# The second half of a block's turned sums: from one VectorE instruction to a ScalarE copy and two GpSimd additions

## The chip, the core and the metric

The kernel runs on one core of a Trainium2 chip. The metric is the device time of one execution in microseconds, of which the median over several runs is taken. A core has five engines that run their own instruction streams side by side: TensorE (PE in the profile; its weight loads have a row of their own, PEld), VectorE (DVE), ScalarE (ACT), GpSimd (POOL) and SyncE (SP), which here only issues DMAs. An engine waits for another by a semaphore.

## What is computed

A decoder layer with three parts, each followed by a row-wise layer normalisation, on x of 16 x 256 rows of 256 numbers, all in float32:

```python
def attn(residual, w_fc, w_proj, ln_g, ln_b):
    x = layernorm(residual, ln_g, ln_b)
    q = x.reshape(Bx, Tx, 4, 64).transpose(0, 2, 1, 3)
    k = w_fc.reshape(-1, 64)
    v = w_proj.T.reshape(-1, 64)
    p = square(relu(einsum('bhtd,sd->bhts', q, k)))
    out = einsum('bhts,sd->bhtd', p, v)
    return residual + out.transpose(0, 2, 1, 3).reshape(Bx, Tx, Cx)
...
x = _layernorm(x + attn(x, ...))
x = _layernorm(x + xattn(x, ctx, fraction, ...))
x = _layernorm(x + ffn(x, ...))
```

The change lies in the first part. Its result before the normalisation is x + (x + out), that is, 2x plus the attention's sums. The second part is an attention of 16 heads over a context, with a bias made from the clipped differences of a fraction; the third a feed-forward layer with eight experts that add a low-rank term. They stay as they are.

## The kernel before, in words

The 4096 rows are cut into NB = 8 blocks of 512. A tile of rows has 128 partitions and four groups of 256 numbers (j = 0 to 3). The order of instructions is written out by hand (`manual_schedule`, from line 949): each engine executes its instructions in the order in which the program issues them.

**Stage one** (lines 973 to 1047, about the first 250 us) is the first part, block after block. In a block TensorE alternates between score steps and values steps. A step m of the eight issues two calls of `scores` (line 334), then the two calls of `values` (line 351) that belong to the scores of the step before, then what the list `steps[m]` holds. A call of `scores` makes four matmuls (eight instructions in the profile, L339) into a ps_a tile, which has two banks of PSUM; ScalarE takes its relu into SBUF (L347), VectorE squares it (L348), and a step later the values matmuls (L358) read it. There are two ps_a buffers, so the relu of one call must have read a buffer before the call after next may write it. Calls of `scores` in a block: 16.

The values are summed in PSUM. `keep` (line 366) takes the sums out after the fourth and the eighth step: a ScalarE copy (L367), another (L372) into `half`, and a GpSimd addition of the two (L373). The sums have channels on the partitions and rows along the free axis; they must be turned.

**The seam between two blocks** is the list `turning` (lines 1004 to 1008, run at 1044): the next block's normalised x is turned in two parts, `turn_in(0)` with a ScalarE eviction (L324) and `turn_in(1)` with a VectorE eviction (L329), and between the two stands `turn_rows` (line 399) for the block before the one that just ended. `turn_rows` takes a ps_a tile, makes two generators of `turn_out` (line 375), one for each half jj of the rows and each with one bank of the tile, and steps them: four transposes for each half (L384), then for each half the eviction at L390, one VectorE instruction that computes 2x + sums from PSUM into y. So the order on TensorE at a seam is: four transposes, eight, four, and the next block's first score step. The seams behind blocks 1 to 6 have a `turn_rows`, for blocks 0 to 5. The seam behind block 0 has none. Blocks 6 and 7 are turned later, in stage two, by `turn_out` without a tile (lines 1088 and 1111).

What reads y: its row statistics in steps 1 and 2 of the next block (`measure_out`, line 406, bn_stats at L185), and `norm_out` (line 410) from step 7 on, a ScalarE scaling into hid (L245) and a GpSimd addition (L413).

The x tiles have three buffers. `nxt.load` in step 0 (line 1001, DMA at L256 on SP's queue) brings the block after into the buffer of the block that was just turned, so it waits until that block's evictions have read x. Behind it on SP's queue stand a row of fractions (L442) and the store of a clipped difference (L553), which VectorE makes at L534 in step 0 and in step 5 of blocks 2 to 6. The loaded x is measured by VectorE in steps 3 and 4.

**Stage two** (from line 1068) runs the attention over the context and the feed-forward part in one hand-made order. The change has no instruction there.

Of the kernel before, what the change touches and what calls it, by code (L numbers as in the profile page):

```python
# [11 lines left out]
ALU = mybir.AluOpType  # L12
# [10 lines left out]
def tile_decoder_layer(ctx: ExitStack, tc: tile.TileContext, a: dict, out: bass.AP):  # L23


    nc = tc.nc
# [23 lines left out]
    def tile_b():  # L50

        if turns:
            turns[0] += 1
            if turns[0] % 3 == 0:
                return psV.tile([P, 512], FP, tag="W", name="ps_b")
        return psB.tile([P, 512], FP, tag="B", name="ps_b")
# [175 lines left out]
    if True:  # L232
# [16 lines left out]
        class Block:  # L249
# [125 lines left out]
            def turn_out(self, jj, ps=None):  # L375
                if self.tb >= NB - 2:
                    self.y = hid[:, 4 * self.tb : 4 * self.tb + 4, :]
                elif jj == 0:
                    self.y = p1.tile([P, 4, C], FP, tag="y", name="y")
                if ps is None:  # L380
                    ps = tile_b()
                for j in range(2):
                    for c in range(CC):
                        nc.tensor.transpose(  # L384
                            ps[:, j * C + c * P : j * C + (c + 1) * P],
                            self.oT[:, c, (2 * jj + j) * P : (2 * jj + j + 1) * P],
                            ident,
                        )
                yield
                nc.vector.scalar_tensor_tensor(  # L390
                    self.y[:, 2 * jj : 2 * jj + 2, :].rearrange("p j c -> p (j c)"),
                    self.x[:, 2 * jj : 2 * jj + 2, :].rearrange("p j c -> p (j c)"),
                    2.0,
                    ps,
                    ALU.mult,
                    ALU.add,
                )
# [551 lines left out]
    with tc.manual_schedule():  # L949
# [23 lines left out]
        for tb in range(NB):  # L973
# [58 lines left out]
            for m in range(8):  # L1032
                c, n2 = divmod(m, 4)
# [34 lines left out]
        for n in range(N + 2):  # L1068
# [135 lines left out]
            if n in measured:  # L1204
                j = measured.index(n)
                row_stats(hid[:, 4 * (NB - 1 - j // 4) + j % 4, :], rest_mv[:, j, :])
            if n in LATE:
                j = LATE.index(n)
# [120 lines left out]
```

## Time and profile before

| | us |
|---|---|
| median of 3 runs | 899.75 (899.52 to 900.03) |
| the profiled execution | 900.11 |
| its span in the trace | 898.3 |
| L348 DVE, squares, 128x1024, x128 | 153.9 busy, 1243 ns mean |
| L390 DVE, evictions into y, 128x512, x12 | 7.7 busy, 684 ns mean |
| L367 and L372 ACT, copies from PSUM, 128x512 | 587 and 592 ns mean |
| L373 POOL, additions, 128x512, x15 | 19.1 busy, 1273 ns mean |
| L413 POOL, additions, 128x256, the 24 of stage one | 723 to 1766 ns, median 1655 |
| POOL busy from 80 to 240 us, by 40 us | 10.2, 11.0, 12.3, 14.6 |

A row of a group gives its line, engine and operation, the tiles that it writes and reads (out<-in), the shape, the count, then busy microseconds and the mean of one in nanoseconds, then the engine's idle time before it and what ended it. A row of the timeline gives the start and the length in microseconds from the span's start; instructions that follow each other closely are merged and counted (x2), and what stands in brackets is the idle time before and its releaser. Score and values steps stand there as x16. The granted TensorE clock is 0.998 of the full one over the execution.

### The profile page before, as it was taken

To read this page: it belongs to the slowest core of one execution; us is meant where nothing else is said; L and a number is where in the kernel's file an instruction comes from. 1 tells how busy PE (TensorE), PEld (TensorE's weight loads), DVE (VectorE), ACT (ScalarE), POOL (GpSimd) and SP (SyncE) were. 2 spreads that over 40 slices of the span, in tenths; PEclk is the share of its full clock that TensorE was granted. 3 is DMA by queue.
4 is the path that set the end of the run, shared out by engine and by line. 5 is a ranking of instruction groups with operands and counts; after the bars stand their busy time and mean duration, and the time that the engine had idled before them with its cause. 6 is when DMAs were issued, how large, how long until landed. Compare 5 with 4: busy or idle time off the path is not lost.

```text
span 898.3 us, 19061 instructions
## 1 busy us (share of the span) xinstructions
PE 887.4 (99%) x6940; PEld 560.8 (62%) x6940; DVE 713.1 (79%) x1986; ACT 567.3 (63%) x951; POOL 398.5 (44%) x385
## 2 busy tenths in 40 slices
PE   8999999999999999999999999999999999999997
PEld 4334444444466777577668757766875786586555
DVE  6879899988779999778777877877798787778344
ACT  5766777777787888376656836666684665556111
POOL 1100223422489998435534644563464456344010
PEclk9999999999999999999999999999999999999999
DMA  5501110110001222011111102011110201111001
GB/s 140 154 1 42 53 42 26 30 49 1 14 1 55 70 69 57 14 42 23 34 49 39 47 14 67 20 37 45 43 48 14 66 20 37 43 28 43 23 2 46
DMA packets 44190, 37.01 MB, mean 41 GB/s; under 512 B 14912, under 2 KB 40000, under 8 KB 44096
## 3 DMA queue, kind: packets, MB, share of 16 engines
q1 hardware_dynamic: 43520, 35.52, 14.5%
q8 instruction: 55, 0.90, 0.4%
q14 instruction: 39, 0.32, 0.1%
q10 hardware_dynamic: 576, 0.26, 0.1%
HBM read 21.07 MB, written 6.03 MB: 30 GB/s over the span
## 4 chain that ended last, share of the span: by engine, by line
PE 97%; DVE 1%; ACT 1%; issue 0%; POOL 0%; DVEq 0%; ACTq 0%; POOLq 0%
PE ps_b L689 13%; PE ps_a L339 13%; PE ps_v L358 12%; PE ps_l L884 12%; PE ps_l L649 8%; PE ps_b L914 7%; PE ps_v L705 7%; PE ps_v L914 5%; PE ps_b L601 3%; PE ps_b L497 3%; PE ps_b L471 3%; PE ps_b L519 3%; PE ps_l L896 2%; PE ps_b L811 1%; PE ps_b L458 1%; PE ps_b L796 1%
## 5 line engine op out<-in xcount | busy, mean ns | idle before, releaser
L628 POOL TENSOR_SCALAR neg<-dneg,aneg,delta 128x512 f32<-128x512 f32 x217 | 182.9, 854 | 181.8 <-PE ps_b L689 127.4
L664 DVE CUSTOM_DVE_ANT_0 neg<-ps_l,neg 128x256 f32<-128x256 f32 x512 | 181.5, 420 | 26.5 <-PE ps_l L649 22.6
L640 ACT ACTIVATE ps_l<-dpos,apos_d 128x512 f32<-128x512 f32 x256 | 172.9, 687 | 40.3 <-DVE mx L664 35.6
L696 ACT ACTIVATE pT<-ps_b 128x512 f32<-128x512 f32 x256 | 142.4, 591 | 59.3 <-PE ps_b L689 57.2
L348 DVE TENSOR_TENSOR pr<-pr 128x1024 f32<-128x1024 f32 x128 | 153.9, 1243 | 30.2 <-ACT pr L347 29.8
L347 ACT ACTIVATE pr<-ps_a 128x1024 f32<-128x1024 f32 x128 | 124.9, 1025 | 52.9 <-PE ps_a L339 52.5
L689 PE MATMUL ps_b<-ident,neg 128*128 128x128 f32 x1024 | 138.5, 277 | 2.0 <-ACT pT L696 1.8
L689 PEld LDWEIGHTS ps_b<-ident,neg 128*128 128x128 f32 x1024 | 113.6, 141 | 35.9 <-issue 12.4
L679 POOL TENSOR_TENSOR neg<-neg,mx 128x1024 f32<-128x1024 f32 x65 | 124.2, 1911 | 18.2 <-DVE mx L664 17.0
L339 PE MATMUL ps_a<-xnT,kT 64*64 64x512 f32 x1024 | 124.6, 593 | 1.0 <-ACT xnT L324 0.4
L358 PE MATMUL ps_v<-pr,vv 64*64 64x512 f32 x1024 | 122.7, 589 | 0.0
L884 PE MATMUL ps_l<-xt,wi 128*128 128x512 f32 x248 | 111.5, 595 | 0.0
L679 DVE TENSOR_TENSOR neg<-neg,mx 128x1024 f32<-128x1024 f32 x63 | 99.2, 1575 | 0.6
L413 POOL TENSOR_TENSOR hid<-hid,bo 128x256 f32<-128x256 f32 x32 | 43.7, 1367 | 105.3 <-ACT hid L245 86.5
L358 PEld LDWEIGHTS ps_v<-pr,vv 64*64 64x64 f32 x1024 | 45.2, 133 | 64.4 <-issue 54.5
L339 PEld LDWEIGHTS ps_a<-xnT,kT 64*64 64x64 f32 x1024 | 42.0, 133 | 65.2 <-issue 52.7
L649 PE MATMUL ps_l<-kM,qT 32*128 32x256 f32 x1024 | 75.9, 401 | 0.0
L884 PEld LDWEIGHTS ps_l<-xt,wi 128*128 128x128 f32 x248 | 45.3, 190 | 49.0 <-issue 44.4
L373 POOL TENSOR_TENSOR xt<-xt,half 128x512 f32<-128x512 f32 x15 | 19.1, 1273 | 120.3 <-ACT half L372 120.3
L914 PE MATMUL ps_b<-wof,hT 128*128 128x256 f32 x304 | 68.4, 380 | 0.0
L705 PE MATMUL ps_v<-pT,vaug 128*32 128x256 f32 x1024 | 66.4, 384 | 0.0
L907 DVE TENSOR_SCALAR hT<-ps_l,wib 128x512 f32<-128x512 f32 x43 | 29.8, 746 | 43.9 <-PE ps_l L896 43.9
(131 smaller groups left out, 1087.3 us busy)
## 6 DMA issues: line engine op xcount, KB each, us to landing
cT<-in_ctxT SPq DMA_DIRECT2D x16, 256.0 KB
kM<-keys SPq DMA_DIRECT2D x128, 32.0 KB
v<-raw SPq DMA_DIRECT2D x128, 32.0 KB
invs<-rows SPq DMA_DIRECT2D x128, 32.0 KB
x<-in_x SPq DMA_DIRECT2D x7, 512.0 KB
out<-x SPq DMA_DIRECT2D x7, 512.0 KB
frow<-in_frac SPq DMA_DIRECT2D x16, 128.0 KB
wi<-in_wiT SPq DMA_DIRECT2D x1, 1024.0 KB
```

Source lines behind the costliest of these rows:

```text
L339: nc.tensor.matmul(sc[64 * k : 64 * k + 64, h, :], lhsT=kT[64 * h : 64 * h + 64, q, hf * P + 64 * k : hf * P + 64 * k + 64], rhs=self.xnT[ ...
L348: nc.vector.tensor_tensor(pr, pr, pr, ALU.mult)
L358: nc.tensor.matmul(self.acc[k][64 * h : 64 * h + 64, :], lhsT=vv[64 * k : 64 * k + 64, hf, 64 * q : 64 * q + 64], rhs=pr[64 * k : 64 * k + ...
L628: nc.gpsimd.tensor_scalar(self.neg[:, g], self.batch.dneg, aneg[:, h : h + 1], delta, ALU.mult, ALU.mult,)
L640: nc.scalar.activation(banks[g], self.batch.dpos.rearrange("p j k -> p (j k)"), AF.Copy, scale=apos_d[:, h : h + 1],)
L649: nc.tensor.matmul(banks[g][:, j * S : (j + 1) * S], lhsT=self.batch.qT[rows, self.o, j * P : (j + 1) * P], rhs=self.batch.kM[rows, self.i ...
L664: nc.vector.tensor_tensor_reduce(out=self.t[:, g, j, :], in0=banks[g][:, j * S : (j + 1) * S], in1=self.neg[:, g, j, :], scale=1.0, scalar ...
L679: eng.tensor_tensor(rows, rows, top.to_broadcast([P, 4, S]), ALU.subtract)
L689: nc.tensor.transpose(ps[:, k * S + j * P : k * S + (j + 1) * P], self.t[:, g, j, k * P : (k + 1) * P], ident,)
L696: nc.scalar.activation(self.pT[:, g, :], self.ps[g], AF.Exp)
L884: nc.tensor.matmul(self.banks[g], lhsT=wi[:, c, f * P : (f + 1) * P], rhs=self.xT[:, c, :], start=(c == 0), stop=False,)
L914: nc.tensor.matmul(ps[:, 0:C], lhsT=self.hT[f][:, j * P : (j + 1) * P], rhs=wof[:, f, :], start=(f == 0), stop=(f == FC - 1),)
```

## The change

`turn_out` remembers whether it took its own PSUM tile. If it was handed one and turns the second half (jj = 1), ScalarE copies the turned sums from PSUM into the two row groups of y, and GpSimd adds x to them twice, in place. The first half, and every call without a tile, keep the VectorE instruction.

```diff
+                own = None
                 if ps is None:
-                    ps = tile_b()
+                    ps = own = tile_b()
                 for j in range(2):
                     for c in range(CC):
                         nc.tensor.transpose(
...
                 yield
+                if ps is not own and jj == 1:
+
+                    rows = self.y[:, 2:4, :].rearrange("p j c -> p (j c)")
+                    nc.scalar.copy(rows, ps)
+                    for _ in range(2):
+                        nc.gpsimd.tensor_tensor(
+                            rows, rows, self.x[:, 2:4, :].rearrange("p j c -> p (j c)"), ALU.add
+                        )
+                    return
                 nc.vector.scalar_tensor_tensor(
                     self.y[:, 2 * jj : 2 * jj + 2, :].rearrange("p j c -> p (j c)"),
                     self.x[:, 2 * jj : 2 * jj + 2, :].rearrange("p j c -> p (j c)"),
```

## The prediction

> **What bounds the kernel now.** I read the page first, then the chain of waits inside stage one, then the timeline around the seams between two blocks of stage one, where the changed lines run.
>
> ```profile
> span 898.3 us, 19061 instructions
> PE 887.4 (99%) x6940; PEld 560.8 (62%) x6940; DVE 713.1 (79%) x1986; ACT 567.3 (63%) x951; POOL 398.5 (44%) x385
> ...
> PE 97%; DVE 1%; ACT 1%; issue 0%; POOL 0%; DVEq 0%; ACTq 0%; POOLq 0%
> ```
>
> TensorE is busy 99% of the span and is 97% of the chain that ended last. So work taken from DVE is worth nothing by itself: only time that TensorE loses counts. A busy PE row can hide such a loss, because the ends of matmuls are modelled. So I compare starts. In the steady part of a block two score steps (x16 in the timeline: eight matmul instructions each) start 1.71 us before the values that follow them (74.08 to 75.79). At a seam it is longer. The seam into the third block, with the turned sums in it:
>
> ```profile
> 70.05 1.29 DVE L390 SCALAR_TENSOR_TENSOR y<-x,ps_a 128x512 f32<-128x512 f32 x2 [0.25 <-PE ps_a L384]
> 70.37 0.21 PEld L339 LDWEIGHTS ps_a<-xnT,kT 64*64 64x64 f32 x8 [0.17 <-issue]
> 70.38 2.19 PE L339 MATMUL ps_a<-xnT,kT 64*64 64x512 f32 x16
> ...
> 71.45 0.24 PEld L339 LDWEIGHTS ps_a<-xnT,kT 64*64 64x64 f32 x8 [0.87 <-issue]
> 71.53 2.12 ACT L347 ACTIVATE pr<-ps_a 128x1024 f32<-128x1024 f32 x2 [1.58 <-PE ps_a L339]
> ...
> 72.36 1.93 PE L358 MATMUL ps_v<-pr,vv 64*64 64x512 f32 x16
> ```
>
> and the seam into the second block, the only one without turned sums:
>
> ```profile
> 37.85 1.95 PE L339 MATMUL ps_a<-xnT,kT 64*64 64x512 f32 x16 [0.43 <-ACT xnT L324]
> ...
> 39.62 1.90 PE L358 MATMUL ps_v<-pr,vv 64*64 64x512 f32 x16
> ```
>
> The reader is to see 72.36 - 70.38 = 1.98 us in the first and 39.62 - 37.85 = 1.77 us in the second: 0.21 us lost. The place is the weight load at 71.45. The seam's tile of turned sums is one of the two ps_a buffers. The block's first score step takes the other, its second this one, and so waits until both L390 evictions have read it. They end at 70.05 + 1.29 = 71.34; the load follows 0.11 us later. The view says "issue" there, but the eviction's end is the only event that fits. The last such seam gives the same (219.21 to 221.19, 1.98). Six seams lose 6 x 0.21 = 1.26 us.
>
> **The change, part by part.** The new branch needs a tile handed in and jj = 1. Only turn_rows hands one in, for blocks 0 to 5: six times. Blocks 6 and 7 call turn_out without one and stay as they are. Each time one DVE L390 goes (684 ns), and one ScalarE copy and two GpSimd additions of 128x512 come.
>
> *Removed, on the path.* With one eviction left DVE ends at 70.05 + 0.68 = 70.73.
>
> *Added, ScalarE.* The nearest row is the copy of 128x512 from PSUM at L372, 592 ns. In program order it stands behind the eviction of turn_in(0) (69.17 + 0.78 = 69.95) and ahead of the relus. It can start when DVE now starts, about 70.06, and ends at 70.65. Behind it waits the relu at 71.53, which sat idle 1.58 us for TensorE: 0.59 of that is filled, 0.9 left. Both readers are done by 70.73, where the second score step would come at about 71.24: cover 0.5 us. The stall of 0.21 goes. Next late is TensorE itself. If ScalarE were 0.6 us later than this, the stall would be back.
>
> *Added, GpSimd.* Two additions like this one:
>
> ```profile
> 74.82 0.59 ACT L372 COPY half<-ps_v 128x512 f32<-128x512 f32 x1
> ...
> 75.49 1.26 POOL L373 TENSOR_TENSOR xt<-xt,half 128x512 f32<-128x512 f32 x1 [16.52 <-ACT half L372]
> ```
>
> It starts 0.08 us after ScalarE's copy, so mine run 70.73 to 72.0 and, with the same 0.08 between them as an estimate, 72.08 to 73.35. The queue ahead is free (an L413 addition ends at 219.2 ahead of the last seam), and the next in it is L373 at 75.49. The rule that speaks against this step is the Trainium skill's, "GPSIMD Engine Reference", section 3.1: an addition there costs about 2.6 cycles per element against VectorE's one, so elementwise work belongs on VectorE. From its 2.6 and 1.2 GHz, 512 elements give an estimate of 1.11 us plus dispatch, near the row's 1.26. As a cost on the path it would be 2 x 1.26 + 0.59 - 0.68 = 2.43 us a seam, 14.6 us in all. By the trace nothing on the path waits for these rows: their readers are the row statistics of measure_out(1) at 82.22, 8.9 us after 73.35. I take zero.
>
> *Moved, the load of x.* The next block's x (512 KB, at 71.40, just after the second eviction) goes into the buffer that the additions read. SP now issues it at about 73.4, 2.0 us later, and with it what stands behind: frow (71.82, read one block later) and nothing urgent, as the store of dneg comes at 75.58. The DMA columns by microsecond show x landed at about 75.1, so it will be about 77.1. Its first reader is at 85.55: 8 us of cover. Zero.
>
> *Shared with DVE.* This is the doubtful part. The squares at L348 run beside the second addition. The rows are
>
> ```profile
> 73.73 1.22 DVE L348 TENSOR_TENSOR pr<-pr 128x1024 f32<-128x1024 f32 x1
> 74.86 0.69 DVE L534 CUSTOM_DVE_ANT_1 dneg<-frow,nfcol 128x512 f32<-128x512 f32 x1
> 76.37 1.47 DVE L348 TENSOR_TENSOR pr<-pr 128x1024 f32<-128x1024 f32 x1 [0.82 <-ACT pr L347]
> ```
>
> and, from the answer on line 413, the spread of an addition of half the size that often meets squares:
>
> ```profile
> L413 POOL TENSOR_TENSOR hid<-hid,bo x24: 723/1655/1766, 98.6 to 251.1; 128x256 f32<-128x256 f32 x24
> ```
>
> The square at 76.37 overlapped L373 by 0.38 us and took about 0.27 longer; L413 goes from 723 to 1655 ns. The Trainium skill, "SBUF — State Buffer", section "Who interferes with whom", says that a VectorE instruction with two SBUF inputs and a GpSimd one that reads SBUF exclude each other: the later one waits until the earlier ends. DVE's remaining L390 and L329 read one operand from PSUM and should not be touched; at 99.81 an L390 beside an L413 shows no lengthening.
>
> After the change the first square is ready at 72.59 and the second addition ends at 73.35. By the rule it waits 0.76; by the row's proportion (0.27 for 0.38) it loses 0.54. It ends at 74.4 to 74.6 and the next at 75.5 to 75.7. Their values matmuls start at 75.58 and 76.44 (0.21 earlier than now): room 1.0 and 0.75. Nothing by either.
>
> In the next step L373 (ready at 75.28, held by the second square until about 75.6) runs to 76.9, the clip at L534 stands ahead of the third square. If the clip is not held, the squares end at 78.0 and 79.15 against values at 79.01 and 79.87. If it is (its two inputs are in SBUF; no row shows one meeting an addition), they end at 78.65 and 79.85: the last has no room, and I put 0.1 us on TensorE. Five seams have a clip, so the cost lies between zero and 0.5 us. I take 0.1, nearer zero, because L373 at 75.49 touched the clip's end and stayed at its own 1.26.
>
> **Sum.** -1.26 + 0.1 = -1.16 us, rounded to -1.2. The profiled execution took 900.11 us (span 898.3 and 1.8 around it): it would become 898.9. The median of the runs shown is 899.75, which gives **898.55 us**. TensorE sets stage two as well, so the shift should reach the end whole.
>
> **Rivals.**
> *The port decides* (slower). The two additions and L373 hold DVE one after another. The place is the fourth square after a seam; from its end to its values matmul there is now 80.08 - 78.98 = 1.10 us, less the 0.11 from an end to a load: 1.0. Up to 0.76 comes from the second addition and 0.3 to 1.0 from L373 and a clip pushed into it: 1.1 to 1.8 in all, and from 1.0 on TensorE stands. In the middle 1.45 - 1.0 = 0.45, and as the stop comes 0.21 earlier, 0.66 us a seam: 5 x 0.66 - 1.26 = +2.0, **901.8 us**. For it: L413 more than doubles beside squares, and DVE has little room in the next steps (two squares 2.36 and two row statistics 1.15 in a step of 3.43). Against: it needs every hold at its end.
> *The stall stays*: the second score step gets another wait, on ScalarE's copy or on two semaphores, as late as the old one. For it: the row was called "issue". Against: the 0.5 us of cover. **899.75 us**.
> *DVE's relief counts in full*: 6 x 0.684 = 4.1 us, **895.6 us**. For it: DVE is at 8 to 9 tenths in stage one. Against: DVE is 1% of the chain.
> That the change does not do what it says is no rival beyond the count: six blocks of eight.
>
> **How the numbers follow.** A measurement of this kernel can tell about 0.2% from no change, 1.8 us: 897.95 and 901.55 are the bounds. My forecast 0.70, all but 0.02 of it within them; the stall stays 0.12, within; DVE's relief 0.05, faster; the port 0.13, slower. So faster 0.07, same 0.80, slower 0.13. The range runs from 897.9 (the forecast and half a microsecond) to 900.3 (the stall stays, with half a microsecond of holds), and leaves out about 0.2.
>
> **What would show it.** Right: at six seams score steps to values in 1.77, not 1.98; the second load no longer behind L390; the copy at 0.59 ended before 71; POOL additions near 1.27, twice six; x issued 2 us later with the statistics unmoved; first squares longer by 0.5 to 0.8. Wrong: values matmuls starting late in the first or second step after a seam (the port), or a second load still 1.08 us behind the first.

## The result, and the profile after

The changed kernel takes **904.0 us** (903.5 to 904.39, five runs) against 899.75 before: a ratio of 1.0048, interval 1.0037 to 1.006. It is slower by 4.25 us, outside the range that was given. The page of the changed kernel, span and busy rows, the chain by engine, the squares, and the addition of `keep`:

```profile
span 902.2 us, 19076 instructions
PE 889.1 (99%) x6940; PEld 548.4 (61%) x6940; DVE 725.4 (80%) x1980; ACT 571.8 (63%) x957; POOL 421.6 (47%) x397
...
PE 89%; DVE 7%; issue 2%; ACT 2%; POOL 0%; DVEq 0%; ACTq 0%; POOLq 0%
...
L348 DVE TENSOR_TENSOR pr<-pr 128x1024 f32<-128x1024 f32 x128 | 164.4, 1326 | 23.7 <-ACT pr L347 23.6
...
L373 POOL TENSOR_TENSOR xt<-xt,half 128x512 f32<-128x512 f32 x15 | 25.7, 1717 | 83.6 <-ACT half L372 83.6
```

VectorE lost six instructions of 684 ns and is nevertheless busy 12.3 us longer: a busy row counts the time in which an instruction is held. The squares went from 1243 to 1326 ns, 10.5 us in all, the addition at L373 from 1273 to 1717. TensorE still reads 99%, but the chain gave 8 points from it to others, 6 of them to VectorE. Of these rows only the chain's says that TensorE now waits for others; the size of the loss is in none of them.

Where it lies is read from the starts of the blocks, the first score step of each on TensorE. Blocks 3 and 4 before:

```profile
100.14 0.66 PE L339 MATMUL ps_a<-xnT,kT 64*64 64x512 f32 x4
...
129.91 0.66 PE L339 MATMUL ps_a<-xnT,kT 64*64 64x512 f32 x4
```

and after:

```profile
99.67 0.66 PE L339 MATMUL ps_a<-xnT,kT 64*64 64x512 f32 x4
...
130.44 0.66 PE L339 MATMUL ps_a<-xnT,kT 64*64 64x512 f32 x4
```

From block 3 to block 7 before: 100.14, 129.91, 159.68, 189.44, 219.21, so 29.77 us each. After: 99.67, 130.44, 161.22, 191.98, 222.75, so 30.77. Block 2 takes 29.74 after, 29.77 before. From the last block's start to the start of the last score call it is 28.24 against 27.66, and what follows takes 651.2 against 651.4. So four blocks lost 1.0 us each and block 7 lost 0.6; block 2 and stage two lost nothing.

The seam into block 2 in the changed kernel, from the timeline (lines of the file moved by one to ten: L400 is the old L390, L544 the clip, L423 the old L413; L394 and L396 are the new copy and the new additions):

```profile
69.60 0.69 DVE L400 SCALAR_TENSOR_TENSOR y<-x,ps_a 128x512 f32<-128x512 f32 x1 [0.25 <-PE ps_a L385]
...
69.93 2.12 PE L339 MATMUL ps_a<-xnT,kT 64*64 64x512 f32 x16
...
70.21 0.80 DVE L329 TENSOR_SCALAR xnT<-ps_b,ln_g,ln_b 128x512 f32<-128x512 f32 x1
...
70.32 0.59 ACT L394 COPY y<-ps_a 128x512 f32<-128x512 f32 x1 [0.81 <-DVE y L400]
...
70.98 3.51 POOL L396 TENSOR_TENSOR y<-y,x 128x512 f32<-128x512 f32 x2 [12.46 <-ACT y L394]
...
71.87 1.90 PE L358 MATMUL ps_v<-pr,vv 64*64 64x512 f32 x16
...
72.14 3.43 DVE L348 TENSOR_TENSOR pr<-pr 128x1024 f32<-128x1024 f32 x2 [1.13 <-ACT pr L347]
...
74.99 1.73 POOL L373 TENSOR_TENSOR xt<-xt,half 128x512 f32<-128x512 f32 x1 [0.49 <-ACT half L372]
...
75.50 1.76 DVE L544 CUSTOM_DVE_ANT_1 dneg<-frow,nfcol 128x512 f32<-128x512 f32 x1
```

Three things are to be seen. First, the copy waits for VectorE's eviction (it ends at 70.29) instead of running beside it. So ps_a is free only at 70.91, 0.98 us behind the block's first score step, where it was 0.96 before (71.34 - 70.38). The seam takes 71.87 - 69.93 = 1.94 us, 0.04 less than before and not 0.21; even this little comes only because the next score call follows the copy's end after 0.05 us, where it followed VectorE's after 0.15. Second, the two additions take 3.51 us, not 2.6: taken one by one the second lasts 2.15, and the two squares 1.23 and 2.29. An instruction is called held here when its row grows to about the end of another engine's instruction that it overlaps. The first square holds the second addition until about 73.3, and that holds the second square until 74.5. Third, the same happens with the next pair: L373 waits for the second square (1.73 for 1.27) and holds the clip (1.76 for 0.69). VectorE is then 2.2 us behind where these instructions alone would put it.

Almost nothing stops in block 2, because the squares had room. The fourth square there, and the values matmuls that read it:

```profile
78.32 1.21 DVE L348 TENSOR_TENSOR pr<-pr 128x1024 f32<-128x1024 f32 x1
```

```profile
79.59 1.08 PE L358 MATMUL ps_v<-pr,vv 64*64 64x512 f32 x8
```

It ends 0.06 us ahead of them, where the kernel before had 1.1. The seam has used up the room, and no more. One step into a later block, block 4, the rows of three engines:

```profile
137.82 1.68 POOL L423 TENSOR_TENSOR hid<-hid,bo 128x256 f32<-128x256 f32 x1 [0.59 <-ACT hid L245]
```

```profile
138.84 1.75 DVE L348 TENSOR_TENSOR pr<-pr 128x1024 f32<-128x1024 f32 x1
```

```profile
140.64 1.09 PE L358 MATMUL ps_v<-pr,vv 64*64 64x512 f32 x8 [0.36 <-DVE pr L348]
```

L423 is the addition of the row bo in `norm_out`, here called a bo addition. It holds the fourth square for 0.53 us, and TensorE waits for that square: here is the stop, 0.54 us against block 2. It is about half of what the block loses. The rest follows in the same way, 0.05 us in the next step and 0.4 in the one behind it:

```profile
145.16 1.70 POOL L423 TENSOR_TENSOR hid<-hid,bo 128x256 f32<-128x256 f32 x1 [3.29 <-ACT hid L245]
```

```profile
148.00 1.09 PE L358 MATMUL ps_v<-pr,vv 64*64 64x512 f32 x8 [0.20 <-DVE pr L348]
```

Blocks 3 to 7 have such additions in steps 1 to 3, block 2 has none. Before the change they cost nothing: block 2 took 29.77 us there as well as the others.

### The profile page after: what moved, and what is told of

Same layout as the page of the kernel before. It is cut to its first block, busy times and chain, and to the rows that moved or that the text cites. A ratio compares the mean times of both kernels' runs of the same rounds, so it can differ in the third digit from the quotient of the medians.

```text
span 902.2 us, 19076 instructions
## 1 busy us (share of the span) xinstructions
PE 889.1 (99%) x6940; PEld 548.4 (61%) x6940; DVE 725.4 (80%) x1980; ACT 571.8 (63%) x957; POOL 421.6 (47%) x397
## 4 chain that ended last, share of the span: by engine, by line
PE 89%; DVE 7%; issue 2%; ACT 2%; POOL 0%; DVEq 0%; ACTq 0%; POOLq 0%
PE ps_b L699 13%; PE ps_l L894 12%; PE ps_v L358 8%; PE ps_a L339 8%; PE ps_l L659 8%; PE ps_b L924 7%; PE ps_v L715 7%; PE ps_v L924 5%; DVE pr L348 4%; PE ps_b L611 3%; PE ps_b L507 3%; PE ps_b L481 3%; PE ps_b L529 3%; PE ps_l L906 2%; PE ps_b L821 1%
## 5 line engine op out<-in xcount | busy, mean ns | idle before, releaser
L348 DVE TENSOR_TENSOR pr<-pr 128x1024 f32<-128x1024 f32 x128 | 164.4, 1326 | 23.7 <-ACT pr L347 23.6
L423 POOL TENSOR_TENSOR hid<-hid,bo 128x256 f32<-128x256 f32 x32 | 37.7, 1180 | 107.0 <-ACT hid L245 88.2
L358 PEld LDWEIGHTS ps_v<-pr,vv 64*64 64x64 f32 x1024 | 38.0, 132 | 76.5 <-DVE pr L348 36.4
L339 PEld LDWEIGHTS ps_a<-xnT,kT 64*64 64x64 f32 x1024 | 37.3, 133 | 69.5 <-issue 50.9
L373 POOL TENSOR_TENSOR xt<-xt,half 128x512 f32<-128x512 f32 x15 | 25.7, 1717 | 83.6 <-ACT half L372 83.6
```

The lines of the kernel that those rows point to most:

```text
L339: nc.tensor.matmul(sc[64 * k : 64 * k + 64, h, :], lhsT=kT[64 * h : 64 * h + 64, q, hf * P + 64 * k : hf * P + 64 * k + 64], rhs=self.xnT[ ...
L348: nc.vector.tensor_tensor(pr, pr, pr, ALU.mult)
L358: nc.tensor.matmul(self.acc[k][64 * h : 64 * h + 64, :], lhsT=vv[64 * k : 64 * k + 64, hf, 64 * q : 64 * q + 64], rhs=pr[64 * k : 64 * k + ...
```

## The experiments

Theory P: the loss comes from GpSimd's additions and VectorE's two-input instructions excluding each other. Its sharper form R: the seam's additions only use up the squares' room; what stops TensorE are the bo additions that then meet late squares. Rivals: S, the copy on ScalarE and its late release; W, GpSimd's work in proportion; B, the backlog of VectorE by itself. In the cuts of code `rows`, `x_rows` and `y_rows` stand for the two row groups of the half in question.

**VectorE adds instead of GpSimd**

```diff
-                    for _ in range(2):
-                        nc.gpsimd.tensor_tensor(rows, rows, x_rows, ALU.add)
+                    nc.vector.scalar_tensor_tensor(rows, x_rows, 2.0, rows, ALU.mult, ALU.add)
```

> The change with its two GpSimd additions replaced by one VectorE instruction (2x + the copied rows, both in SBUF); the ScalarE copy stays. Theory P (the loss comes from GpSimd's additions and VectorE's squares shutting each other out of SBUF): no L373 and no clip longer than before, squares back at 1243 ns mean, no stop of TensorE at values; the seam from scores to values stays at the changed kernel's 1.94 us against 1.98, so 899.75 - 6 x 0.04 = 899.5 us. Theory S (the copy on ScalarE and its later release of ps_a cost the time): still about 904.

Measured: 900.9 us, ratio 1.0014 (1.0007 to 1.0021). The copy stayed and most of the loss is gone, so S does not hold, but it is 1.4 us over what P expected. Blocks 3 to 6 take 30.18. Its rows in step 1 of block 3, GpSimd and VectorE, each from its engine's timeline:

```profile
106.44 0.72 POOL L423 TENSOR_TENSOR hid<-hid,bo 128x256 f32<-128x256 f32 x1 [0.95 <-ACT hid L245]
```

```profile
106.49 1.75 DVE L348 TENSOR_TENSOR pr<-pr 128x1024 f32<-128x1024 f32 x1
```

and the same two in the kernel before:

```profile
107.58 1.76 POOL L413 TENSOR_TENSOR hid<-hid,bo 128x256 f32<-128x256 f32 x1 [1.05 <-ACT hid L245]
```

```profile
107.54 1.21 DVE L348 TENSOR_TENSOR pr<-pr 128x1024 f32<-128x1024 f32 x1
```

Before, the square comes 0.04 us ahead and GpSimd waits (1.76), which costs nothing, as nobody waits for that row. Here the addition comes 0.05 ahead and the square is held to 1.75. The clip had delayed L373 by 0.1, that the third square, that the fourth: 0.1 us decides which side pays. This square still had room (1.02 us, now 0.48). The next two bo additions hold a square in the same way, and only there TensorE stops, by 0.05 and 0.43 us. The second stop:

```profile
116.02 1.09 PE L358 MATMUL ps_v<-pr,vv 64*64 64x512 f32 x8 [0.20 <-DVE pr L348]
```

**The same without the bo additions of steps 1 to 3**

```diff
-                eng.tensor_tensor(rows, rows, bo, ALU.add)
+                if eng:
+                    eng.tensor_tensor(rows, rows, bo, ALU.add)
```

> The run with the VectorE addition in place of GpSimd's (900.9 us) without the bo additions to row groups 1 to 3 in steps 1 to 3 (those rows lack bo). That run lost 0.41 us in each of blocks 3 to 6, where its fourth square was held 0.53 us by a bo addition that in the kernel before comes 0.04 us too late to hold it. Theory R: without these additions its blocks take 29.70 us, about 899.1 us. If the VectorE addition itself costs the time: 900.9 stays.

Measured: 899.2 us, ratio 0.9996 (0.9987 to 1.0004); the blocks take 29.70. The 1.7 us between the two runs belong to the bo additions' holds.

**One addition** (the second half's rows lack one x)

```diff
-                    for _ in range(2):
+                    for _ in range(1):
```

> The change with one GpSimd addition of x instead of two, so that the second half's rows are x + sums and not 2x + sums. Theory P by place: the one addition runs from 70.98 to 72.25, the first square comes at 72.14, so nothing is held but 0.1 us; time as in the run with the VectorE addition, 899.5 us. Theory W (GpSimd's work costs in proportion): half of the 4.25 us stays, about 901.9 us.

Measured: 899.0 us, ratio 0.9993 (0.9984 to 1.0001). W falls: half of the work costs none of the loss. The timelines of GpSimd and VectorE show the single addition ending about as the first square begins, and both squares at their own length:

```profile
100.69 1.28 POOL L396 TENSOR_TENSOR y<-y,x 128x512 f32<-128x512 f32 x1 [1.04 <-ACT y L394]
```

```profile
101.85 2.36 DVE L348 TENSOR_TENSOR pr<-pr 128x1024 f32<-128x1024 f32 x2 [1.13 <-ACT pr L347]
```

**Two further additions in the kernel before**

```diff
+                if own is None and jj == 1:
+                    spare = p1.tile([P, 2 * C], FP, tag="spare", bufs=1, name="spare")
+                    nc.gpsimd.tensor_tensor(spare, y_rows, x_rows, ALU.add)
+                    nc.gpsimd.tensor_tensor(spare, spare, x_rows, ALU.add)
```

> The kernel before, both evictions on VectorE, with two further GpSimd additions of 128x512 into a spare tile after each of the six seams; nothing reads the result. Theory P: the second addition waits for the first square and then holds the second one, L373 is held by that and holds the clip, as in the changed kernel: 904 to 905 us, squares at a mean near 1326 ns. Theory S (the ScalarE copy and the y that comes late cost the time): nothing waits for the spare tile, about 900 us.

Measured: 905.6 us, ratio 1.0066 (1.005 to 1.0083), squares at 1331 ns. With both evictions on VectorE, and nothing waiting for the results, the additions cost 6.0 us. P stands without the copy.

**The change without the bo additions of steps 1 to 3**

```diff
-                        lambda j=j, tb=tb: older.norm_out(by[tb - 1], 4 + j, j, nc.gpsimd)
+                        lambda j=j, tb=tb: older.norm_out(by[tb - 1], 4 + j, j, None)
```

with the edit of `norm_out` as above.

> The change without the GpSimd additions of bo to row groups 1 to 3 of the blocks that get them in steps 1 to 3 of a block (those rows lack bo). Theory R (the seam's two additions only push VectorE late by some 1.4 us at the fourth square; what stops TensorE for 1.0 us in each of blocks 3 to 6 and 0.6 in block 7 are the bo additions that now hold late squares): every block after the second takes 29.74 us as block 2 does in the changed kernel, 904.0 - 4.6 = 899.4 us. Theory B (VectorE's backlog alone stops TensorE): 903 to 904 us.

Measured: 899.0 us, ratio 0.9994 (0.9985 to 1.0003); blocks 29.73 to 29.75. The seam is held as in the changed kernel, VectorE's rows at one of them:

```profile
132.02 3.44 DVE L348 TENSOR_TENSOR pr<-pr 128x1024 f32<-128x1024 f32 x2 [1.13 <-ACT pr L347]
135.38 1.75 DVE L545 CUSTOM_DVE_ANT_1 dneg<-frow,nfcol 128x512 f32<-128x512 f32 x1
```

yet nothing of the loss is left: 5.0 us less than the changed kernel. R holds against B: the backlog of the seam alone stays within the squares' room, with 0.06 us left at the fourth square. It costs 29.74 against the 29.70 of the run with one addition. The load of x is as late as in the changed kernel (4.59 us behind the start of block 4 in both), so that is not the cause either.

**The clip moved out of step 0**

```diff
-        slots = [(tb, m) for tb in range(2, 7) for m in (0, 5)]
+        slots = [(tb, m) for tb in range(2, 7) for m in (5, 6)]
```

> The change with the clip of step 0 moved into step 6 (clips in steps 5 and 6). The clip no longer stands between the second and the third square, where L373 held it for 1.07 us; L373 then holds the third square instead, to about 76.75. Theory R: the fourth square ends about 0.5 us earlier than now but is still held by a bo addition, so part of the stops stays: 901 to 902.5 us. If the clip's hold is all that counts: 899.5 us. If it is nothing: 904.

Measured: 904.0 us, ratio 1.0049 (1.0032 to 1.0066). A miss: R had expected 901 to 902.5. The fourth square of block 4 ends at 139.97, 0.16 ahead of its values, so there the clip's absence helped as reckoned; but bo additions hold later squares in steps 2 and 3. And the clip in step 6 delays the squares of step 7, whose last one the bo addition there then holds to 1.75, and with it the eviction at the next seam: the last block's second score call comes 1.66 us behind its first. So moving the clip made new meetings; the clip was one link and not the cause.

**The copy into a tile of its own, VectorE adds later**

```diff
-                    nc.scalar.copy(rows, ps)
-                    for _ in range(2):
-                        nc.gpsimd.tensor_tensor(rows, rows, x_rows, ALU.add)
+                    self.half = p1.tile([P, 512], FP, tag="half", bufs=1, name="half")
+                    nc.scalar.copy(self.half, ps)
...
                turning.append(lambda: nxt.turn_in(1))
+                if tb:
+                    turning.append(rows_in[tb - 1].add_rows)   # y = 2x + half, on VectorE
```

> ScalarE copies the second half's sums into the tile half, and one VectorE instruction adds 2x and the copy into y after the eviction of turn_in(1); no GpSimd addition. Tests the gain that the prediction counted, and why ScalarE's copy began only when VectorE's first eviction had ended (70.32 against 70.29). If both writing y tied them: the copy starts near 70.06, ps_a is free at 70.73, the seam takes 1.77 us, 899.75 - 1.26 = 898.5 us. If the shared PSUM tile ties them: the copy still starts with the eviction's end, the seam stays at 1.94, about 899.5 us.

Measured: 899.4 us, ratio 0.9997 (0.9988 to 1.0005). Rows of VectorE and ScalarE:

```profile
98.70 0.69 DVE L396 SCALAR_TENSOR_TENSOR y<-x,ps_a 128x512 f32<-128x512 f32 x1 [0.24 <-PE ps_a L385]
```

```profile
99.47 0.59 ACT L394 COPY half<-ps_a 128x512 f32<-128x512 f32 x1 [0.87 <-DVE y L396]
```

The copy writes nothing that VectorE's eviction touches, and still waits for it. What the two share is the ps_a tile. It is not PSUM as a whole: in the changed kernel's seam VectorE's L329 reads ps_b from 70.21 to 71.01 while the copy reads ps_a from 70.32.

**Each half turned and evicted before the next**

```diff
-                for half in halves * 2:
-                    next(half, None)
+                for half in halves:
+                    for _ in range(2):
+                        next(half, None)
```

> The kernel before with the two halves of turn_rows one after the other: four transposes, their eviction, four transposes, their eviction, both evictions on VectorE as before. No GpSimd work. If an eviction needs only its own half's transposes: VectorE starts at about 69.6, ends at about 70.97, the second score step no longer waits, 899.7 - 1.2 = 898.5 us. If the halves of one PSUM tile are kept apart in time, the second four transposes wait for the first eviction: some 0.8 us more in each of six seams, about 904 us.

Measured: 906.8 us, ratio 1.0084 (1.0069 to 1.0099). TensorE's row at a seam:

```profile
70.62 0.66 PE L384 MATMUL ps_a<-ident,xt 128*128 128x128 f32 x4 [0.88 <-DVE y L390]
```

The second half's transposes wait for the first half's eviction. Two engines do not work on the halves of one ps_a tile at a time, as this program is built. The time is 2.8 us over what was expected for that: block 2 takes 30.62, blocks 3 to 6 take 31.23, and the squares have a mean of 1291 ns, so holds have their part in it.

**The copy first**

```diff
-                for half in halves * 2:
+                for half in halves + halves[::-1]:
```

> The change with ScalarE's copy of the second half issued ahead of VectorE's eviction of the first. The copy then starts when the transposes end, as the prediction assumed, and both additions are in line ahead of the first square: the second runs from about 2.15 to 3.4 us after the block's first score step has begun, less than the first square's start at 2.2. If the prediction's reckoning was right but for the late copy: the first square is held 0.6 to 0.8 us, nothing stops, 899 to 900 us. Theory R (any hold in step 0 pushes L373 into the clip, and late squares then meet bo additions): again 903 to 904 us.

Measured: 902.0 us, ratio 1.0029 (1.0019 to 1.0039). Now the copy starts when the transposes end, as the prediction had it. GpSimd and VectorE at the seam into block 4:

```profile
130.33 2.63 POOL L396 TENSOR_TENSOR y<-y,x 128x512 f32<-128x512 f32 x2 [0.24 <-ACT y L394]
135.05 1.28 POOL L373 TENSOR_TENSOR xt<-xt,half 128x512 f32<-128x512 f32 x1 [2.09 <-ACT half L372]
```

```profile
132.21 2.97 DVE L348 TENSOR_TENSOR pr<-pr 128x1024 f32<-128x1024 f32 x2 [0.52 <-ACT pr L347]
135.10 1.78 DVE L544 CUSTOM_DVE_ANT_1 dneg<-frow,nfcol 128x512 f32<-128x512 f32 x1
```

The additions have their reckoned length, the first square is held 0.6 us, as reckoned. But L373 holds the clip for 1.09, and bo additions meet the late squares: blocks 3 to 6 take 30.47. Better by 2 us than the change, worse by 2.6 than the kernel before.

**The stall removed in another way**

```diff
                     coming.append((now, c, n, now.scores(c, n)))
+                    if tb > 1 and m == 0 and n == 0:
+                        block, *args = behind.pop(0)
+                        block.values(*args)
```

> The kernel before, evictions as before, with the first of the two values calls of a seam's step 0 moved between the two score calls (six seams). The second score call then comes 0.86 us later, after the evictions' end at 71.34, so the stall of 0.21 us goes; its square also comes about 0.65 us later. If nothing else moves: 899.6 - 1.2 = 898.4 us. If the later square sets L373 and the clip against each other and then a bo addition against the fourth square (theory R, the lock goes to whoever comes first): the gain is lost, 900 to 902 us.

Measured: 902.4 us, ratio 1.0031 (1.0021 to 1.0042). Block 2 takes 29.52, so the stall of about 0.2 us is real and this removes it. Blocks 3 to 6 take 30.43: GpSimd's and VectorE's rows show the clip held once more, with no GpSimd instruction added.

```profile
134.81 1.35 POOL L373 TENSOR_TENSOR xt<-xt,half 128x512 f32<-128x512 f32 x1 [4.85 <-ACT half L372]
```

```profile
134.94 1.77 DVE L534 CUSTOM_DVE_ANT_1 dneg<-frow,nfcol 128x512 f32<-128x512 f32 x1
```

**One addition with the whole result**

```diff
+                elif jj == 1:
+                    nc.scalar.activation(self.y[:, 2:4, :], self.x[:, 2:4, :], AF.Copy, scale=2.0)
...
-                    nc.scalar.copy(rows, ps)
-                    for _ in range(2):
-                        nc.gpsimd.tensor_tensor(rows, rows, x_rows, ALU.add)
+                    nc.scalar.copy(half, ps)
+                    nc.gpsimd.tensor_tensor(rows, rows, half, ALU.add)
```

> The change with one GpSimd addition and the whole result: ScalarE writes 2x into y ahead of the copy, copies the sums into the tile half, GpSimd adds the two once. If the second addition is what costs (one addition gave 898.99 with x + sums): about 899.2 us, a little over that for 0.6 us more on ScalarE in each seam. If one GpSimd addition with the right data costs as much as two: 902 and more.

Measured: 899.3 us, ratio 0.9997 (0.9988 to 1.0006). The idea of the change without its loss; it can't be told from the kernel before. No version run here, with the whole result, is clearly faster than that.

## Why the prediction was wrong, point by point

- *The bound.* TensorE bounds the kernel, and only what it loses counts: right. The stall of 0.21 us a seam behind the evictions: right, shown by block 2 of the run with the values between (29.52 for 29.77).
- *Removed, on the path; added, ScalarE.* Wrong in one term: the copy "can start when DVE now starts". It starts when VectorE's eviction ends, so 0.69 + 0.59 follow each other as 0.69 + 0.68 did, and ps_a comes free no sooner (0.98 us behind the first score step, 0.96 before). The gain of 1.26 us was not there: at most some 0.07 us a block (29.70 with one addition).
- *Added, GpSimd.* The lengths were right for additions that meet nothing (1.27), and that nobody waits for the rows. With the late copy the second one met the first square and took 2.15.
- *The load of x.* Later than reckoned, 74.52 and not 73.4, as the second addition ended at 74.49; but right in its cost, as nobody waited.
- *Shared with DVE.* **The step that failed.** The prediction took 0.1 us from a range of zero to 0.5, and its reckoning ended with the fourth square. The choice for the clip was wrong: it rested on a row that touched the clip's end only, and where the addition is already running the clip is held (1.75 to 1.78 in four runs, 0.69 alone). But that choice alone cost next to nothing. The prediction's other branch, with the clip held, put the fourth square's end 0.02 us ahead of its values; block 2 shows 0.06, and the run without bo additions pays 0.04 us a block. What it put at nothing without a reason are the bo additions of steps 1 to 3, whose row it had itself shown as lengthening from 723 to 1655 ns. Those 0.9 us were GpSimd waiting. Squares that come later turn the same meeting round, and then TensorE pays: 1.0 us in each of four blocks, 0.6 in the last. The copy-first run separates this from the late copy: with the copy where the prediction had it, 902.0.
- *The rule of the Trainium skill* ("SBUF — State Buffer", "Who interferes with whom") that the later one waits to the other's end fits these runs better than the row's proportion. The second square at the seam overlaps the addition by 1.20 us and is held 1.09; the fourth square of block 4 overlaps by 0.67 and is held 0.54. Each wait ends some 0.12 us ahead of the addition's recorded end. So does the row that the prediction read as a proportion, 0.27 of 0.38. The page's sentence that the order of issue decides who blocks is what the pair with 0.04 and 0.05 us shows.
- *Rivals.* "The port decides" named the holding, priced 901.8 and was given a chance of 0.13. Its chain at the seam came true up to the fourth square, and there used up the room and no more: the run without bo additions has that whole chain and loses nothing. The bo additions are not in it, so its price of five seams at 0.66, where four blocks lost 1.0 and one 0.6, would have been luck had it come closer. "The stall stays" came true as well, as a part.
- *Sum.* -1.2 was forecast; measured +4.25: about -0.2 at the seams, +4.7 from the stops, stage two unmoved; the 0.25 between that sum and the medians is within what single executions differ by. The run without bo additions takes 5.0 of it away. The lower bound of the range, 897.9, is 0.65 below the forecast and not the half microsecond that it names; nothing hangs on it.

What stays open: whether bo additions placed elsewhere would let the removed stall pay was not tried. Block 2's 29.52 for 29.77, times six seams, gives an estimate of 1.5 us.

## What to carry to other kernels

An engine that looks idle is not free if its instructions and a busy engine's hold each other: ask for each instruction put there which instruction of the other engine it will meet, and who waits for that one. A row that is long only because it waits costs nothing yet, but is a warning: a shift of 0.1 us can hand the wait to the other side. And moving an instruction to another engine gives no overlap if both still work on one tile that the program keeps to one engine at a time.

## What the runs showed of the hardware that was not expected

A GpSimd addition that is waiting gets in between two VectorE squares that follow each other without a gap: 1.23 and 2.29 us for two that take 2.36 together alone. So a run of VectorE instructions is no protection; each boundary between two of them is a place where a waiting addition can take over. The VectorE instruction that clips, with its two inputs read by broadcasting from SBUF, is held like the squares (0.69 to 1.77). The held time is counted as busy on both engines: VectorE's row rose by 12.3 us with six instructions fewer.
